# Gathered rows in one ring of 42, freed row by row, in place of seven buffers of six; the column products inside the next tile's sum

## The chip, the cores and the metric

The kernel runs on one core of a Trainium2 chip. The metric is the device time of one execution in microseconds (us); less is better. Engines are called by the profile's names: PE is TensorE (matmul; PEld is its weight load), DVE is VectorE, ACT is ScalarE, POOL is GpSimd, SP is SyncE.

## The reference

Two graph layers on 3327 nodes with 512 features; the adjacency matrix is random, symmetric, with some nine ones in a row. Cut to what matters:

```python
# layer 0: graph attention with 4 heads of 128 features
feats = einsum('nf,hfo->hno', x, W)
logits = lrelu(e_s[:, :, None] + e_n[:, None, :], 0.2) - 1e10 * (1 - adj)
out = relu(softmax(logits) @ feats + b)          # heads side by side
x1 = layernorm(x + out)
# layer 1: an attention sum and a plain sum over the same neighbours
gate_a = sigmoid([adj @ x1, x1] @ Wa.T + ba);  gate_b = sigmoid([adj @ x1, x1] @ Wb.T + bb)
e = where(adj != 0, exp(-leaky_relu(s_left[:, None] + s_right[None, :], 0.01)), 0)
x_a = (e / (sum(e) + 1e-5)) @ (x1 @ W_sa);  x_b = adj @ (x1 @ W_g) + b_g
out = layernorm(x1 + sigmoid(gate_a * x_a + gate_b * x_b))
```

## The kernel before

As few entries of the adjacency matrix are set, the kernel doesn't multiply by it. It has three stages.

**Lists (up to about 213 us).** It reads the matrix once, makes for each node a list of its neighbours' numbers, computes the features of all nodes into a table in HBM (`table0`, rows of 520 floats: 512 features and 8 more), and sorts the nodes by their number of neighbours, in two groups of 12 and 14 tiles of 128 nodes. So each tile `j` has a cap `CAPS[j]` on the neighbours of its nodes, from 14 down to 4. The first tile of a group (`T0`: tiles 0 and 12) has one row more, the "stair", for the few nodes with longer lists.

**Layer 0 (213 to 547 us).** For each tile, a gather is one indirect DMA on POOL's queue that brings one neighbour's row for each of the 128 nodes: 128 rows of 2080 bytes, 266 KB. `gather(table, j)` issues those of a whole tile. The rows go to buffers of `U` = 6 rows each, of which there are `GB` = 7 under one tag; a tile takes one to three of them, filled evenly, so that many are not full. In the second group a tile's first place is the node's own input row, fetched as a pair with its own table row from `own1` by one DMA. A buffer is given to a new tile once all reads of all its rows are done.

The tiles run in the order `order0`: 11, 10, 0 to 9, 23, 12, 24, 13, 22, 14, 21, 15, 20, 16, 19, 17, 18, 25. Step `i` of the loop at line 884 issues, in this order (each engine runs its own part in order, and the waits between engines and DMAs follow from the data):

- the gathers of the tile three steps ahead (`AHEAD`, line 887)
- `publish` of finished tiles, in groups of up to four: they are scaled by ACT and, with DVE's columns, written to `table1`, in the second group by a scatter on POOL's queue
- `columns2` of the tile two steps back: ACT copies its transposed row (`xt1`, line 842), and PE makes eight columns of products from it (`pcol`, line 845)
- `attend` of this tile: each gathered row is multiplied by its weights in place, two rows of three on DVE (line 815), every third (`s % 3 == 2`) on ACT (line 813), and PE adds it up in PSUM with an identity matrix (line 821)
- for the tile one step back: the sum plus input (line 899), transposes on PE (`columns1`, line 838), statistics for the layer norm; then `columns3`, the copy of the columns on DVE (line 849)
- `weigh_a` and `weigh_b` of the next tile: logits, softmax. Line 770 adds the logits' two parts and line 787 copies the neighbours' new numbers, each once for every part (buffer) of the tile, `got[j]`.

**Layer 1 (from 550 us).** The same with `table1`, in another order of tiles (short ones first, then long and short in turn, the two shortest last). Here DVE makes the weighted sum (line 1026) and adds some rows in pairs (line 1028, `paired`, counted within a part); PE adds rows and pairs (line 1047), turns the sums (line 1057) and multiplies them by the two weight matrices (line 1066). `weights_a` has one line 961, one line 970 and, after the first, one line 981 for each part of the tile. Finished rows are scattered to the output on POOL's queue (line 145) in groups.

Of the kernel before, what the change touches and what calls it, by code (L numbers as in the profile page):

```python
# [8 lines left out]
F32 = mybir.dt.float32  # L9
# [5 lines left out]
P = 128  # L15
# [9 lines left out]
S = 24  # L25
# [4 lines left out]
LW = 32  # L30
ND = 25
LEVELS = 4
U = 6
GB = 7
AT = 12
NCOL = 8
GRP = 4
# [42 lines left out]
def sparse_pass(  # L80
# [39 lines left out]
    nc = tc.nc  # L120
# [521 lines left out]
    m0 = tc.alloc_tile_pool(name="m0", bufs=2, side="left")  # L642
    ps = ctx.enter_context(tc.tile_pool(name="ps", bufs=1, space=PSUM))

    def gather(table, j):


        g, i = place(j)
        ahead = 0 if table is table1 else 1 + g
        c = CAPS[j] + ahead  # L650
        more = j in T0
        n = (c + more + U - 1) // U
        w = (c + more + n - 1) // n
        got = []
        for q0 in range(0, c + more, w):
            m = min(w, c - q0)
            buf = gp.tile([P, U, ROW], F32, tag="g", name=f"g_{nc.next_id()}", bufs=GB)
            for q in range(q0, q0 + m):
                s = q - ahead + 1
                if ahead == 2 and q < 2:  # L660
                    if q == 0:
                        nc.gpsimd.indirect_dma_start(
                            out=buf[:, 0:2, :].rearrange("p t w -> p (t w)"), out_offset=None,
                            in_=own1.rearrange("n t w -> n (t w)"),
                            in_offset=bass.IndirectOffsetOnAxis(ap=srt[g][:, i, S + 1 : S + 2], axis=0),
                        )
                    continue
                nc.gpsimd.indirect_dma_start(  # L668
                    out=buf[:, q - q0, :], out_offset=None, in_=table[:, :],
                    in_offset=bass.IndirectOffsetOnAxis(ap=srt[g][:, i, s : s + 1], axis=0),  # L670
                )
            o = 1 if ahead == 2 and q0 == 0 else 0
            if m > o:
                got.append((q0 + o - ahead + 1, m - o, buf, o))
        if more:
            stair[j] = buf[:, m, :]
            nc.gpsimd.indirect_dma_start(
                out=stair[j], out_offset=None, in_=table[:, :],
                in_offset=bass.IndirectOffsetOnAxis(ap=ids2[g][:, 0:1], axis=0),
            )  # L680
        return got

    stair = {}

    def to_nodes(pool, psum, name, cols):

# [72 lines left out]
        few, many = few[1:], many[1:]  # L759
    order0 += second[-1:]  # L760
    assert sorted(order0) == list(range(NT))
    got, ws, accs, ws2 = {}, {}, {}, {}

    def weigh_a(j):
        c = slots(j)
        g, i = place(j)
        w = ws[j] = m0.tile([P, S + 1, H], F32, tag="w", name=f"w{j}", bufs=3)
        es = srt[g][:, i : i + 1, S + 2 : S + 2 + H].bitcast(F32)
        for s0, n, buf, o in got[j]:
            nc.vector.tensor_add(w[:, s0 : s0 + n, :], buf[:, o : o + n, F : F + H], es.to_broadcast([P, n, H]))  # L770
        if j in T0:
            logit = m0.tile([P, H], F32, tag="logit", name=f"logit{j}")
            nc.vector.tensor_add(logit, stair[j][:, F : F + H], es2[g])
            small = psx.tile([P, B * H], F32, tag="pcol", name=f"to_nodes{j}", bufs=2)
            nc.vector.tensor_tensor(
                w[:, C0 + 1 :, :], to_nodes(m0, small, f"n{j}", logit),
                no_step.rearrange("p (b o) -> p b o", o=1).to_broadcast([P, B, H]), ALU.add,
            )
        nc.vector.scalar_tensor_tensor(w[:, :c], w[:, :c], 0.2, w[:, :c], ALU.mult, ALU.max)
        mx = m0.tile([P, 1, H], F32, tag="mx", name=f"mx{j}")  # L780
        nc.vector.tensor_reduce(mx[:, 0, :], w[:, :c].rearrange("p s h -> p h s"), AX.X, ALU.max)
        nc.vector.tensor_sub(w[:, :c], w[:, :c], mx.to_broadcast([P, c, H]))  # L782
        nc.scalar.activation(w[:, :c], w[:, :c], AF.Exp)  # L783

        for s0, n, buf, o in got[j]:
            a = max(s0, 1)
            nc.scalar.copy(srt[g][:, i, a : s0 + n], buf[:, o + a - s0 : o + n, F + H])
        if j in T0:
            nc.scalar.copy(ids2[g], stair[j][:, F + H : F + H + 1])
# [8 lines left out]
            small = psx.tile([P, B * H], F32, tag="pcol", name=f"to_rows{j}", bufs=2)  # L798
            ws2[j] = to_rows(m0, small, f"n{j}", w[:, C0 + 1 :, :])

    def attend(j, lean):


        w = ws[j]
        acc = accs[j] = ps.tile([P, F], F32, tag="acc", name=f"acc{j}", bufs=2)
        if not lean:
            nc.tensor.matmul(acc, ident, bias0, start=True, stop=False)
        for s0, n, buf, o in got[j]:
            for s in range(s0, s0 + n):
                gv = buf[:, o + s - s0, 0:F].rearrange("p (h o) -> p h o", h=H)  # L810
                if s % 3 == 2:
                    for h in range(H):
                        nc.scalar.activation(gv[:, h, :], gv[:, h, :], AF.Copy, scale=w[:, s, h : h + 1])  # L813
                else:
                    nc.vector.tensor_tensor(  # L815
                        gv, gv, w[:, s, :].rearrange("p (h o) -> p h o", o=1).to_broadcast([P, H, FO]), ALU.mult
                    )
                row = buf[:, o + s - s0, 0:F]
                if lean and s == 0:
                    nc.vector.tensor_add(row, row, bias0)  # L820
                nc.tensor.matmul(  # L821
                    acc, ident, row, start=(lean and s == 0), stop=(s == CAPS[j] and j not in T0)
                )
        if j in T0:
            gv = stair[j][:, 0:F].rearrange("p (h o) -> p h o", h=H)
            nc.vector.tensor_tensor(
                gv, gv, ws2[j].rearrange("p (h o) -> p h o", o=1).to_broadcast([P, H, FO]), ALU.mult
            )
            nc.tensor.matmul(acc, to_node, stair[j][:, 0:F], start=False, stop=True)
# [5 lines left out]
    def columns1(j):  # L835
        pt = turned[j] = psx.tile([P, KT, P], F32, tag="pt", name=f"x1t{j}", bufs=2)
        for k in range(KT):
            nc.tensor.transpose(pt[:, k, :], row1(j)[:, k * P : (k + 1) * P], ident)

    def columns2(j):  # L840
        xt1 = m0.tile([P, KT, P], F32, tag="xt1", name=f"xt1_{j}")
        nc.scalar.copy(xt1, turned[j])  # L842
        pcol = psx.tile([P, B * H], F32, tag="pcol", name=f"pcol{j}", bufs=2)[:, :NCOL]
        for k in range(KT):
            nc.tensor.matmul(pcol, xt1[:, k, :], v1[:, k, :], start=(k == 0), stop=(k == KT - 1))  # L845
        turned[j] = pcol
# [14 lines left out]
        else:  # L861
            scatter("table1", table1[:, :], own(j), row1(j), N - 1)

    AHEAD = 3
    for i in range(AHEAD):
        got[order0[i]] = gather(table0, order0[i])
    nc.sync.dma_start(own1[:, 0, :], xo)
    nc.sync.dma_start(own1[:, 1, :], table0[NG[0] * P : NP, :])
    psl.release()
# [12 lines left out]
    weigh_b(order0[0])  # L882
    ready = [[], []]
    for i in range(NT + 3):
        if i + AHEAD < NT:
            j = order0[i + AHEAD]
            got[j] = gather(table0, j)
        for args in ready[0]:
            publish(*args)
        ready = [ready[1], []]  # L890
        if 2 <= i < NT + 2:
            columns2(order0[i - 2])
        if i < NT:
            attend(order0[i], i >= 3)
        if 0 < i <= NT:
            j = order0[i - 1]
            y = row1(j)[:, 0:F]
            xj = y if j < NG[0] else got[j][0][2][:, 0, 0:F]
            nc.vector.scalar_tensor_tensor(y, accs[j], 0.0, xj, ALU.max, ALU.add)
            columns1(j)  # L900
            done = norm.add(i - 1, y)
            if done:
                k0, scale, shift = done
                ready[1] = [
                    (order0[k], scale[:, k - k0 : k - k0 + 1], shift[:, k - k0 : k - k0 + 1]) for k in range(k0, i)
                ]
        if 2 <= i < NT + 2:
            columns3(order0[i - 2])
        if 0 < i <= 7:
            sort1(rankis[1], 2 * i - 2, 2 * i)  # L910
        if i == 8:
# [156 lines left out]
    ends = {3, 7, 11, 15, 19, 22, 24, 25}  # L1068
    norm = Norm(m1, "n1", ends)
    at_ = lambda i: order[i] if 0 <= i < NT else None  # L1070
    for i in range(3):
        got[at_(i)] = gather(table1, at_(i))
    own_score(at_(0))
    weights_a(at_(0))
    weights_b(at_(0))
# [1 line left out]
    ready = None  # L1077
    for i in range(NT + 3):
        j, j1, jp, jpp = at_(i), at_(i + 1), at_(i - 1), at_(i - 2)
        if at_(i + 3) is not None:  # L1080
            got[at_(i + 3)] = gather(table1, at_(i + 3))
        if j1 is not None:
            own_score(j1)
        if jp is not None:
# [491 lines left out]
```

## Time and profile before

| | |
|---|---|
| median of 3 runs | 951.75 us (950.07 to 954.26) |
| the profiled execution | 953.83 us, its span 951.8 us |
| PE | 793.3 us busy, 83% of the span |
| DVE | 742.8 us, 78% |
| ACT | 279.0 us, 29% |
| POOL | 612.6 us, 64% |
| gathers of one row (line 668) | 464, 1035 ns each, 3.8 us from issue to landing |
| gathers of a pair (line 662), of a stair (line 677) | 14, 4 |
| granted PE clock, mean | 0.908 of full speed |

Shares of busy time are means over stages with different limits, so each stage has to be read by itself: the busy times in a stretch of time, the waits of one engine in it, and the timeline of that engine. In a row of groups the columns are: line, engine, operation, output and inputs, how often; then busy time in us and the mean of one in ns; then the idle time of the engine ahead of them, with what ended it ("issue" is idle time that no recorded event explains). In a timeline the columns are start in us, length in us, engine, line, operation, how often, and in brackets the idle time before it and what ended it. In a list of waits they are: who waited for whom, us in total, times, longest.

### The profile page before, as it was taken

What the parts mean: (1) busy time and instruction counts of PE and PEld (TensorE: products, weight loads), DVE (VectorE), ACT (ScalarE), POOL (GpSimd) and SP (SyncE); (2) the same over time, 40 slices, a digit from 0 to 9 for tenths busy, and PEclk for the clock granted to TensorE, in tenths of its full rate; (3) what the DMA queues carried; (4) which work ended last, traced back from release to release, by engine and by line L of the source; (5) the groups of instructions that cost most, each with busy time, mean ns of one, the idle gap of its engine ahead of it and who ended that gap; (6) DMA issues with size and microseconds to landing.
All of it is one profiled execution on the core that took longest, in us unless ns stands there. A gap on an engine that the chain in (4) does not pass through costs nothing.

```text
span 951.8 us, 10098 instructions
## 1 busy us (share of the span) xinstructions
PE 793.3 (83%) x2516; PEld 418.3 (44%) x2516; DVE 742.8 (78%) x2175; ACT 279.0 (29%) x820; POOL 612.6 (64%) x654
## 2 busy tenths in 40 slices
PE   4698987338999797799959749999989989899893
PEld 3476764114455444344434414444444434344341
DVE  4386888886987597487757839799999989999873
ACT  1121221004253254235343412213231222222241
POOL 6710154776677767767777477777777777777511
PEclk9798997558999898989989959999999999999997
DMA  8999899998678777877777266777676676667401
GB/s 334 374 366 396 336 328 391 383 384 282 180 201 256 211 237 225 299 240 226 225 223 232 106 179 190 200 188 190 190 197 190 189 192 192 190 188 188 138 23 47
DMA packets 71986, 221.41 MB, mean 233 GB/s; under 512 B 12912, under 2 KB 16960, under 8 KB 71024
## 3 DMA queue, kind: packets, MB, share of 16 engines
q0 software_dynamic: 46560, 153.64, 54.5%
q1 hardware_dynamic: 22704, 64.94, 18.0%
q10 hardware_dynamic: 2656, 2.10, 0.7%
q8 instruction: 23, 0.38, 0.2%
q14 instruction: 43, 0.35, 0.1%
HBM read 199.78 MB, written 28.32 MB: 240 GB/s over the span
## 4 chain that ended last, share of the span: by engine, by line
PE 44%; DVE 15%; DMA 15%; POOL 11%; issue 10%; ACT 3%; DVEq 0%; SPq 0%; POOLq 0%; ACTq 0%
PE acc L821 19%; PE pf L369 9%; POOL g L668 9%; DMA g<-table,srt 8%; DVE sw L1026 6%; PE po L1066 5%; DMA at<-in_adjB 5%; PE acc L1047 4%; PE pcol L845 2%; DVE g L1028 2%; DMA at<-in_adjL 1%; POOL out L145 1%; DMA a_row<-in_a_self 1%; PE sorted L548 1%; ACT za L1111 1%
## 5 line engine op out<-in xcount | busy, mean ns | idle before, releaser
L668 POOL DMA_INDIRECT g<-table,srt x464 | 480.2, 1035 | 159.0 <-issue 122.8
L821 PE MATMUL acc<-g,ident 128*128 128x512 f32 x504 | 239.1, 632 | 2.7 <-DVE g L815 1.6
L1026 DVE SCALAR_TENSOR_TENSOR sw<-g,e,sw 128x512 f32<-128x512 f32 x226 | 169.4, 750 | 12.4 <-ACT sw L1010 8.2
L821 PEld LDWEIGHTS acc<-g,ident 128*128 128x128 f32 x504 | 100.4, 203 | 123.8 <-issue 89.2
L1047 PE MATMUL acc<-g,ident 128*128 128x512 f32 x262 | 128.0, 617 | 23.0 <-DVE g L1028 13.3
L369 PE MATMUL pf<-w,xc 128*128 128x260 f32 x416 | 103.5, 412 | 13.6 <-DVE w L309 13.6
L815 DVE TENSOR_TENSOR g<-g,w 128x512 f32<-128x512 f32 x176 | 112.0, 694 | 0.6
L369 PEld LDWEIGHTS pf<-w,xc 128*128 128x128 f32 x416 | 84.7, 206 | 29.9 <-DVE w L309 14.1
L1066 PE MATMUL po<-wg,sT 128*128 128x512 f32 x208 | 96.6, 608 | 0.0
L1066 PE MATMUL po<-wsa,sT 128*128 128x512 f32 x208 | 94.7, 598 | 0.3 <-ACT sT L1059 0.3
L813 ACT ACTIVATE g<-g,w 128x128 f32<-128x128 f32 x304 | 91.6, 389 | 0.7 <-DVE w L796 0.7
L1047 PEld LDWEIGHTS acc<-g,ident 128*128 128x128 f32 x262 | 49.7, 195 | 93.6 <-issue 44.4
L1028 DVE TENSOR_TENSOR g<-g 128x512 f32<-128x512 f32 x95 | 65.7, 692 | 3.3
L379 POOL DMA_DIRECT2D table<-row x26 | 14.4, 553 | 80.1 <-ACT st L378 80.1
L1096 ACT ACTIVATE za<-za 128x512 f32<-128x512 f32 x26 | 16.4, 631 | 161.0 <-DVE za L1094 161.0
L1066 PEld LDWEIGHTS po<-wg,sT 128*128 128x128 f32 x208 | 40.7, 197 | 51.8 <-issue 50.8
L1066 PEld LDWEIGHTS po<-wsa,sT 128*128 128x128 f32 x208 | 40.0, 193 | 51.0 <-issue 48.5
L145 POOL DMA_INDIRECT out<-za,srt x26 | 29.1, 1121 | 49.3 <-ACT za L1111 43.3
L397 PE MATMUL pc<-at,pow 128*32 128x512 bf16 (+1 forms) x182 | 24.8, 412 | 40.8 <-DMA at<-in_adjB 24.6
L845 PE MATMUL pcol<-v,xt 128*128 128x8 f32 x208 | 29.8, 270 | 31.2 <-ACT xt L842 31.2
L783 ACT ACTIVATE w<-w 128x40 f32<-128x40 f32 (+10 forms) x26 | 6.2, 237 | 149.5 <-DVE w L782 149.5
L845 PEld LDWEIGHTS pcol<-v,xt 128*128 128x128 f32 x208 | 28.4, 209 | 37.8 <-ACT xt L842 36.6
(252 smaller groups left out, 931.6 us busy)
## 6 DMA issues: line engine op xcount, KB each, us to landing
at<-in_adjB SPq DMA_DIRECT2D x78, 512.0 KB, 11.7
g<-table,srt POOLq DMA_INDIRECT x464, 3.8
table<-row POOLq DMA_DIRECT2D x26, 260.0 KB, 6.3
xc<-in_xB SPq DMA_DIRECT2D x6, 1024.0 KB, 8.4
own<-in_xo SPq DMA_DIRECT2D x1, 3640.0 KB, 32.2
own<-table SPq DMA_DIRECT2D x1, 3640.0 KB, 48.7
at<-in_adjL SPq DMA_DIRECT2D x13, 256.0 KB, 13.3
table<-x1a SPq DMA_DIRECT2D x12, 260.0 KB, 4.2
```

Source lines behind the costliest of these rows:

```text
L145: put = nc.gpsimd.indirect_dma_start(out=dst, out_offset=bass.IndirectOffsetOnAxis(ap=rows, axis=0), in_=src, in_offset=None, bounds_check ...
L369: nc.tensor.matmul(pf[:, hh, :HC], xc[:, k, o : o + P], w0[:, k, hh, :], start=(k == 0), stop=(k == KT - 1))
L397: nc.tensor.matmul(pc[32 * c : 32 * c + 32, : nt * P], pow2[:, s, :], loaded[i, m], start=(s == 0), stop=(m + 1 not in ms or s == 3),)
L668: nc.gpsimd.indirect_dma_start(out=buf[:, q - q0, :], out_offset=None, in_=table[:, :], in_offset=bass.IndirectOffsetOnAxis(ap=srt[g][:, i ...
L813: nc.scalar.activation(gv[:, h, :], gv[:, h, :], AF.Copy, scale=w[:, s, h : h + 1])
L815: nc.vector.tensor_tensor(gv, gv, w[:, s, :].rearrange("p (h o) -> p h o", o=1).to_broadcast([P, H, FO]), ALU.mult)
L821: nc.tensor.matmul(acc, ident, row, start=(lean and s == 0), stop=(s == CAPS[j] and j not in T0))
L845: nc.tensor.matmul(pcol, xt1[:, k, :], v1[:, k, :], start=(k == 0), stop=(k == KT - 1))
L1026: nc.vector.scalar_tensor_tensor(sw, g[:, i, 0:F], e[:, s : s + 1], sw, ALU.mult, ALU.add)
L1028: nc.vector.tensor_add(g[:, i, 0:F], g[:, i - 1, 0:F], g[:, i, 0:F])
L1047: nc.tensor.matmul(plain[j], to, row, start=(not sums_of_two and i == 0), stop=(sums_of_two and i == len(rows) - 1),)
L1066: nc.tensor.matmul(proj[j], sT[:, k, :], wt[:, k, :], start=(half + k == 0), stop=(half + k == KT))
```

## The change

The seven buffers become one tile of 42 rows, `ring`. `plan` is called ahead for all tiles of a layer: it gives each row the next place, so that a tile's rows lie in one stretch, in two where the ring's end cuts it, and a pair never wraps (a place is left out for that). It puts the row's gather on a list. `gather()` issues gathers from that list as long as the row's place belonged to a tile that was freed; `free(j)` marks all rows up to tile `j` as free. Both are called in a step after the sum of the tile one step back is taken (in layer 1 at the head of the step). On the chip a gather still waits for the reads of the row that its place held before.

`columns2` is cut in two: ACT's copy (`columns2a`) stays ahead of `attend`, PE's products go into `attend`, behind the matmul of row 2.

```diff
-U = 6
-GB = 7
+RING = 42
...
-    def gather(table, j):
...
+    got, stair = {}, {}
+    ring = gp.tile([P, RING, ROW], F32, name="ring")
+    planned, freed = [0], [0]
+    waiting, ends_at = [], {}
...
+    def plan(table, j):
         g, i = place(j)
...
+        own_x_too = table is table0 and g == 1
+        first = 1 if table is table1 else 0
+        got[j] = []
+        s = first
+        while s <= CAPS[j]:
+            n = 2 if own_x_too and s == 0 else 1
+            if planned[0] % RING + n > RING:
+                planned[0] += 1
+            p = planned[0] % RING
+            m = min(CAPS[j] + 1 - s + n - 1, RING - p)
+            buf = ring[:, p : p + m, :]
+            got[j].append((s, m - (n - 1), buf, n - 1))
...
+            for k in range(k, m):
+                planned[0] += 1
+                waiting.append((planned[0], buf[:, k, :], table[:, :], srt[g][:, i, s : s + 1]))
+                s += 1
...
+        ends_at[j] = planned[0]
+
+    def gather():
+
+        while waiting and waiting[0][0] - freed[0] <= RING:
+            indirect(*waiting.pop(0)[1:])
+
+    def free(j):
+
+        freed[0] = ends_at[j]
...
-    def attend(j, lean):
+    def attend(j, lean, between):
...
                 nc.tensor.matmul(
                     acc, ident, row, start=(lean and s == 0), stop=(s == CAPS[j] and j not in T0)
                 )
+                if s == 2:
+                    between()
...
+    def columns2a(j):
+        xt1s[j] = m0.tile([P, KT, P], F32, tag="xt1", name=f"xt1_{j}")
+        nc.scalar.copy(xt1s[j], turned[j])
+
     def columns2(j):
-        xt1 = m0.tile([P, KT, P], F32, tag="xt1", name=f"xt1_{j}")
-        nc.scalar.copy(xt1, turned[j])
+        xt1 = xt1s[j]
...
-    AHEAD = 3
-    for i in range(AHEAD):
-        got[order0[i]] = gather(table0, order0[i])
+    for j in order0:
+        plan(table0, j)
+    gather()
...
     for i in range(NT + 3):
-        if i + AHEAD < NT:
-            j = order0[i + AHEAD]
-            got[j] = gather(table0, j)
         for args in ready[0]:
             publish(*args)
         ready = [ready[1], []]
-        if 2 <= i < NT + 2:
-            columns2(order0[i - 2])
+        third = order0[i - 2] if 2 <= i < NT + 2 else None
+        if third is not None:
+            columns2a(third)
         if i < NT:
-            attend(order0[i], i >= 3)
+            attend(order0[i], i >= 3, lambda: third is None or columns2(third))
+        elif third is not None:
+            columns2(third)
         if 0 < i <= NT:
...
             nc.vector.scalar_tensor_tensor(y, accs[j], 0.0, xj, ALU.max, ALU.add)
+            free(j)
+            gather()
             columns1(j)
...
-    for i in range(3):
-        got[at_(i)] = gather(table1, at_(i))
+    for j in order:
+        plan(table1, j)
+    gather()
...
-        if at_(i + 3) is not None:
-            got[at_(i + 3)] = gather(table1, at_(i + 3))
+        if i > 0 and jp is not None:
+            free(jp)
+        gather()
```

More of the change, by code (lines that the diff above doesn't have):

```diff
@@ L643, in sparse_pass @@
     ps = ctx.enter_context(tc.tile_pool(name="ps", bufs=1, space=PSUM))
-    def gather(table, j):
-        g, i = place(j)
[L649 to L681, printed above, removed]
@@ L683, in sparse_pass, with indirect @@
-    stair = {}
+    got, stair = {}, {}
+    ring = gp.tile([P, RING, ROW], F32, name="ring")
+    planned, freed = [0], [0]
+    waiting, ends_at = [], {}
+    def indirect(out_, table, ap):
+        nc.gpsimd.indirect_dma_start(
+            out=out_, out_offset=None, in_=table, in_offset=bass.IndirectOffsetOnAxis(ap=ap, axis=0)
+        )
+    def plan(table, j):
+        g, i = place(j)
+        own_x_too = table is table0 and g == 1
[10 more added lines that the diff above has]
+            got[j].append((s, m - (n - 1), buf, n - 1))
+            k = 0
+            if n == 2:
+                both = buf[:, 0:2, :].rearrange("p t w -> p (t w)")
+                planned[0] += 2
+                waiting.append((
+                    planned[0], both, own1.rearrange("n t w -> n (t w)"), srt[g][:, i, S + 1 : S + 2]
+                ))
+                k, s = 2, 1
+            for k in range(k, m):
+                planned[0] += 1
+                waiting.append((planned[0], buf[:, k, :], table[:, :], srt[g][:, i, s : s + 1]))
+                s += 1
+        if j in T0:
+            stair[j] = ring[:, planned[0] % RING, :]
+            planned[0] += 1
+            waiting.append((planned[0], stair[j], table[:, :], ids2[g][:, 0:1]))
+        ends_at[j] = planned[0]
@@ L761, in sparse_pass @@
     assert sorted(order0) == list(range(NT))
-    got, ws, accs, ws2 = {}, {}, {}, {}
+    ws, accs, ws2 = {}, {}, {}
     def weigh_a(j):
@@ L786, in weigh_a @@
             a = max(s0, 1)
+            if a == s0 + n:
+                continue
             nc.scalar.copy(srt[g][:, i, a : s0 + n], buf[:, o + a - s0 : o + n, F + H])
@@ L838, in columns1 @@
             nc.tensor.transpose(pt[:, k, :], row1(j)[:, k * P : (k + 1) * P], ident)
+    xt1s = {}
+    def columns2a(j):
+        xt1s[j] = m0.tile([P, KT, P], F32, tag="xt1", name=f"xt1_{j}")
+        nc.scalar.copy(xt1s[j], turned[j])
     def columns2(j):
-        xt1 = m0.tile([P, KT, P], F32, tag="xt1", name=f"xt1_{j}")
-        nc.scalar.copy(xt1, turned[j])
+        xt1 = xt1s[j]
         pcol = psx.tile([P, B * H], F32, tag="pcol", name=f"pcol{j}", bufs=2)[:, :NCOL]
```

## The prediction

> **What bounds the kernel now.** I read the busy table by stretches first, then GpSimd's waits in layer 0, its timeline, and the chain of waits. Layer 0's sums run from 213 to 547 us, layer 1's from 550 to 940. The busy times of three stretches (length, then PE, PEld, DVE, ACT, POOL, clock, DMA share, GB/s):
>
> ```profile
> 213.00:340.00 127.00, 118.06 (x334) 59.01 (x335) 97.23 (x271) 50.99 (x174) 89.37 (x90) 0.93 0.76 224
> 460.00:547.00 87.00, 68.25 (x216) 35.30 (x214) 62.29 (x199) 33.34 (x99) 58.82 (x59) 0.93 0.63 194
> 680.00:800.00 120.00, 113.32 (x307) 52.45 (x306) 111.52 (x256) 32.11 (x75) 93.98 (x86) 0.99 0.69 191
> ```
>
> TensorE fills the first stretch (118 of 127), nothing fills the second, TensorE and VectorE both fill the third. POOL looks idle everywhere, but a gather costs more than its busy time: each starts 0.30 us after the last ended, even when it waits for nothing. The groups of costliest instructions:
>
> ```profile
> L668 POOL DMA_INDIRECT g<-table,srt x464 | 480.2, 1035 | 159.0 <-issue 122.8
> ```
>
> So a row of gather costs 1.035 + 0.30, about 1.3 us (1.25 undisturbed), while TensorE sums a row in 0.86 (28 products in 12.0 us). Over layer 0 POOL is the slower one, and what it loses is not won back. What it lost there, by its waits between 173 and 547 us (total, times, longest):
>
> ```profile
> POOL g L668 <- PE acc L821: 9.5, 10, 4.3
> POOL g L668 <- DVE x1b L899: 5.5, 2, 3.1
> POOL g L668 <- ACT x1a L853: 4.4, 1, 4.4
> ```
>
> Less 0.30 each these are 6.5 + 4.9 + 4.1, with one odd gap of 0.35 about **15.8 us**, all waits for a buffer of six rows, at 216, 238, 336, 380, 404 and 410 us; none comes after 413. The chain of waits from 459 us on shows who pays:
>
> ```profile
> 515.54 3.94 DMA g<-table,srt
> ...
> 522.54 0.70 DVE g L820
> 523.29 8.85 PE acc L821 x20
> ```
>
> The last gather of tile 18 lands, its weights follow, and the sum starts: from here to the end of layer 0 everything hangs on that landing. Two tiles earlier it is the same (landing at 494, sum at 500). In layer 1 POOL loses only 2.6 us at the start; its gathers run at the 0.30 spacing from 550 to 889 us.
>
> **What the Trainium skill says.** "Perfetto Trace Analysis", section Optimization Strategy: a gap that repeats can mean that there is no room for the next tile. Here the trace agrees: the gaps above end with a reader that frees a buffer. The same page, Identifying Dependency Chains: an instruction that waits on several engines may get extra EventSemaphore instructions ahead of it. The trace has 91 of them before the 464 gathers of L668, most of 17 or 43 ns when nothing is late. "DMA: Bandwidth & Descriptors", Anatomy of one DMA, gives 2.0 us + bytes/436e3, for a gather of 266 KB an estimate of 2.6 us; the trace has 3.8 from issue to landing, which I use.
>
> **The change, part by part.**
>
> *Ring.* A row's gather waits for the row 42 places earlier. Take POOL's times of before less its waits, and TensorE's times of before as the release: ring row 42 would be gathered near 226, its place is free at 215; row 71 near 265, free at 253; row 107 (tile 8) near 310, free at 292; row 174 (tile 14) near 392, free at about 376. POOL trails by 8 us or more each time, so it never waits: -15.8 us of POOL's path by 413 us. Nothing is added to the gathers but waits (below).
>
> *Order on POOL.* Gathers are now issued after the sum of the step, up to 42 rows past the tile just freed, and publish's scatters of that step stand before them. Steps 18 and 22 scatter four tiles each. Before, the second four stood behind the last gather (523 us). Now they stand ahead of the last two or three rows of tile 18 and those of tile 25: the rows past tile 20 are 12 (tile 16) + 10 (19) + 11 (17) = 33, so only 9 of the 11 of tile 18 are issued by then (with places lost at wraps, fewer). Four scatters take 5.2 us (473.74 to 478.96). Their data come from a publish that follows the weights of tile 19, whose gathers land 15.8 earlier too, at 479; POOL gets to them near 497: no wait. So tile 18's last gather lands 15.8 - 5.2 = **10.6 us earlier**. SP's queue only has the two copies into own1 behind 42 instead of 29 first gathers, which another queue issues: nothing.
>
> *Column products.* TensorE stood 31.2 us before pcol (L845). Typical pieces of its timeline:
>
> ```profile
> 421.57 0.60 PE L838 MATMUL x1t<-ident,x1b 128*128 128x128 f32 x4
> 422.90 1.06 PE L845 MATMUL pcol<-v,xt 128*128 128x8 f32 x8 [0.73 <-ACT xt L842]
> ```
>
> After the change rows 0 and 1 (1.71 us) fill the 0.73; but row 2 is scaled by ScalarE after the same copy: copy 0.58 + four of 0.31, ready 1.97 after the transposes. 0.26 remains, so 0.47 a tile is saved, on some 14 tiles (in the five with sort1's products there was no gap): 6 us of TensorE. In tiles that wait for weights, pcol used to run during that wait; its 0.9 us now lie inside the sum. VectorE gets its columns (L849) three rows later, about 2 us, and the next tile's weights are queued behind: tiles of 5 to 8 rows may give 1 us each back. As TensorE waits for gathers at the end, all this cancels to nothing, except in tile 18, where the 0.9 is on the path and 0.5 comes back at tile 25. Layer 0: -10.6 + 0.4 = **-10 us**; if the scatters land behind tile 18, -15; if TensorE's losses reach the end, -5.
>
> *One stretch.* A layer 1 tile came in up to three parts, each with its own L961, L970 and all but the first L981 (49, 49 and 25 less 2 for the stairs). Laid out in 42 places there are 31 parts: 18 fewer. The rows say 0.22 + 0.16 + 0.16 us of busy time; start to start it is about 0.45: 18 x 0.45 = 8 us of VectorE, which sets the pace (111.5 of 120). But gathers come just in time: in the twelfth tile (tile 0, 14 rows) the last one lands 1.3 us before its weights, so of the 4 us saved up to there only 1 is kept; after it 8 parts, 3.6 us, are kept (later leads are 3.5 to 10 us). Layer 1: **-4 us**, from 0 to -8. Layer 0 loses 26 of 55 L770 (0.18 us) and as many casts, hidden by the wait for TensorE. Pairs stay at 95.
>
> *Waits, not shown before.* Each gather now waits for its own row's readers, so two or three semaphore waits may precede every gather. At nothing: the first gather of a buffer starts 0.30 after the last with its wait as without, as does a scatter, whose EVENT_SEMAPHORE and MOVE precede it (the one at 475.07 starts 0.30 after the one before). They run while the last gather is generated, 0.95 us. The other bound is in line: 2 x 43 ns x 482 gathers = +41 us; below zero nothing, as no wait is removed that cost anything but the 15.8. I take 0.
>
> **Sum.** -10 - 4 = -14. The profiled execution took 953.83 (span 951.8), so 939.8; it lies 2.1 above the median 951.75, which gives **938**, with 929 to 946 for this case.
>
> **Rivals.**
> 1. *The gain is smaller or gone*: POOL waits elsewhere, for the scatters' data or because TensorE, with VectorE's later columns, becomes the pace: against it, TensorE at full pace from 400 us on has 204 products of 0.43 and ten tiles' 1.6 us of the rest up to the end of tile 18, near 505, or 510 with VectorE's delays, instead of 532. Two scatter waits of 5 us take 10 away: 948.
> 2. *Slower: semaphores in line on POOL.* Price above, +41 us of POOL, which sets layer 0 (254 gathers, 22 us) and has 1 to 10 us of lead in layer 1. Against the 14 it decides from 0.03 us a gather. For it: every gather gets them; against: the constant 0.30. +41 - 14 = 27: 979.
> 3. *The change doesn't do row by row*: waits are kept for the ring as a whole, and each tile's weights wait for gathers two tiles ahead. A tile then takes its gathers (12 us), landing and sum (14) in turn, 26 x 12 us or so more in one layer: over 1200. Against it: x1a is also one tile with many rows, and L899 on one row waits for TensorE alone.
> 4. *More*: scatters fall behind tile 18 and layer 1 keeps its 8 us: -23, 929.
>
> **Chances.** Forecast 0.64, rival 1 0.14, rival 2 0.14, rival 3 0.03, rival 4 0.05. Range 929 to 954: it leaves out rivals 2 and 3 and takes in rival 1 with the time of before. About 0.5% (4.8 us) can be told from no change. Faster by more: 0.71; within: 0.11; slower: 0.18.
>
> **What would show it.** POOL's waits on L821, L899 and L853 in layer 0 gone; four scatters near 498, ahead of the last gathers; the last gather ends near 512 instead of 522.7; layer 1's first gather near 540 instead of 550.4; the wait of L845 below 10 us; L961 31 times. Wrong: a gap over 0.35 between POOL's gathers, POOL waiting at the first scatter of a step, or TensorE waiting on VectorE's products in tiles of 5 to 8 rows.

## The result, and the profile after

The changed kernel takes **946.21 us** (median of 11 runs, 944.53 to 947.82) beside 951.75 of the kernel before on the same chip: a ratio of 0.9942, 95% interval 0.9918 to 0.9965. It is 5.5 us faster, where 14 were forecast. The profiled execution took 945.74 us, its span 943.7. The spans of the two traces differ by 8.1 us, more than the medians: 0.8 of that lies ahead of layer 0's first sum, and the trace of the kernel before is 2.1 slower than its median.

Two marks split the span: the last gather of layer 0 (the one of tile 25's last row, on POOL) and the first gather of layer 1. Absolute times of two traces can't be compared in layer 0, since TensorE's first sum there starts anywhere from 207.9 to 212.6 us in the traces of this study; so I count from that sum. In us:

| | first sum to last gather | last gather to layer 1's first | layer 0 together | layer 1 to the end |
|---|---|---|---|---|
| before | 311.8 | 28.6 | 340.4 | 401.4 |
| after | 308.6 | 31.6 | 340.2 | 394.4 |
| forecast, after less before | -10.6 | +0.4 | -10 | -4 |
| measured, after less before | -3.2 | +3.0 | -0.2 | -7.0 |

So **the whole gain is layer 1's, and layer 0 gives nothing** that can be told. Three kernels below share the changed kernel's layer 0, instruction for instruction; theirs lasted 339.3, 339.3 and 342.1 us, so one trace tells layer 0 to about 1.5 us. Five share its layer 1, which lasted 393.8 to 394.4 us in four of them and 397.2 in the fifth.

First GpSimd's waits of the changed kernel, from 173 to 547 us (who waited for whom, us in total, times, longest):

```profile
POOL ring L650 <- issue: 37.5, 123, 0.3
POOL ring L650 <- DMA ring<-table,srt: 16.8, 55, 0.3
POOL ring L650 <- PE acc L835: 14.0, 46, 0.3
POOL ring L650 <- DVE x1b L920: 11.4, 2, 9.5
POOL table L144 <- DVE x1b L878: 10.3, 1, 10.3
POOL table L144 <- DVE shifted L877: 10.1, 1, 10.1
```

The old waits are gone: what is left behind PE or ScalarE is the 0.30 us between any two gathers. But a new one is there, 11.4 us in two pieces, 10.8 without the two times 0.30 (6.7 to 10.2 in the three other traces of this layer 0): gathers that wait for line 920, the residual sum (line 899 before). The two waits of L144 at the end are scatters behind the last gather, which wait for their data; the kernel before has 11.1 us of those. POOL's timeline of the changed kernel at the new wait:

```profile
380.91 0.94 POOL L650 DMA_INDIRECT ring<-table,srt  x1 [9.49 <-DVE x1b L920]
382.16 0.95 POOL L650 DMA_INDIRECT ring<-table,srt  x1 [0.30 <-PE acc L835]
...
391.66 0.94 POOL L650 DMA_INDIRECT ring<-table,srt  x1 [1.89 <-DVE x1b L920]
```

VectorE's timeline says what it waited behind:

```profile
372.62 0.68 DVE L829 TENSOR_TENSOR ring<-ring,w 128x512 f32<-128x512 f32 x1
373.33 0.69 DVE L834 TENSOR_TENSOR ring<-ring,bias 128x512 f32<-128x512 f32 x1
373.94 5.50 DVE L829 TENSOR_TENSOR ring<-ring,w 128x512 f32<-128x512 f32 x9
379.36 0.68 DVE L842 TENSOR_TENSOR ring<-ring,w_n 128x512 f32<-128x512 f32 x1
379.96 0.68 DVE L920 SCALAR_TENSOR_TENSOR x1b<-acc,ring 128x512 f32<-128x512 f32 x1
```

Line 920 of tile 23 adds that tile's own input row, which lies in the ring as the first half of its pair. PE had finished the tile's sum by 366.8 (its transposes for the tile before start there), but the step's program has VectorE do all the products of tile 12, the longest one, ahead of line 920. So the place of that one row stays taken to 380.6, and every later gather is behind the one that wants it. The kernel before stands for the same sum at nearly the same time, 172.6 us after the first sum and 171.8 in the changed one:

```profile
382.56 0.94 POOL L668 DMA_INDIRECT g<-table,srt  x1 [3.06 <-DVE x1b L899]
```

At this gather, the 152nd, the changed kernel's GpSimd was 16.3 us ahead of the kernel before, counted from the first sum. Five gathers later, behind its own wait, it is 7.5 ahead.

POOL's timeline at the end of layer 0, the scatters first and then the last gather of all:

```profile
503.71 1.02 POOL L144 DMA_INDIRECT table<-x1b,srt  x1 [0.30 <-issue]
...
507.64 0.98 POOL L144 DMA_INDIRECT table<-x1b,srt  x1 [0.30 <-issue]
...
517.75 0.94 POOL L650 DMA_INDIRECT ring<-table,srt  x1 [0.30 <-issue]
```

The four scatters stand ahead of tile 18's last rows and wait for nothing, as forecast. At the last gather ahead of them GpSimd is 8.5 us ahead of the kernel before, at the first one behind them 3.3: they cost 5.2. TensorE there, in the kernel before (the transposes of tile 17) and then in the changed one:

```profile
520.78 0.60 PE L838 MATMUL x1t<-ident,x1b 128*128 128x128 f32 x4
```

```profile
510.52 0.60 PE L854 MATMUL x1t<-ident,x1b 128*128 128x128 f32 x4
519.64 5.13 PE L835 MATMUL acc<-ring,ident 128*128 128x512 f32 x6 [8.52 <-DMA ring<-table,srt]
```

TensorE now reaches tile 18 early (tile 17's transposes at 510.52, before at 520.78) and waits 8.5 us for rows. Its first six products then take 5.13 us, at a mean granted clock of 0.53; six of the kernel called both below, after a wait of 3.01, take 2.84 at a clock of 1.00. That is 2.3 us on the path, and with the column products' 0.8, now inside this sum, it is about the 3.0 us by which the tail grew. The slow start is the larger part of it: in the kernel called columns_whole below, which has the column products ahead of the sum, the tail is 32.0 us as well, and the sum's 20 products take 11.40 us in place of 8.85.

Of the gathers' semaphores, the trace of after has (duration in ns: least, median, most):

```profile
L650 POOL DMA_INDIRECT ring<-table,srt x464: 940/947/1508, 170.6 to 885.2; - x155
L650 POOLq EVENT_SEMAPHORE  x445: 17/17/4009, 166.7 to 877.7; - x149
```

445 where there were 91, and the spacing of the gathers is still 0.30.

Layer 1 has two parts. Up to tile 13's scores (the sixth tile) VectorE waits for gathers, and that start is as long as before: 62.3 us from layer 1's first gather, 61.4 after. From there on the length follows VectorE's work. Its timelines of before and of after at that point, the last score of tile 13:

```profile
612.63 0.23 DVE L961 TENSOR_SCALAR e<-g,x1b 128x3 f32<-128x3 f32 x1 [4.79 <-DMA g<-table,srt]
```

```profile
610.68 0.23 DVE L984 TENSOR_SCALAR e<-ring,x1b 128x13 f32<-128x13 f32 x1 [3.94 <-DMA ring<-table,srt]
```

From these to the ends of the spans it is 339.2 us before and 333.0 after. The busy times of these two stretches (length; PE, PEld, DVE, ACT, POOL), before and then after:

```profile
613.00:952.00 339.00, 307.98 (x830) 143.28 (x828) 298.09 (x722) 96.26 (x221) 227.53 (x208) 0.96 0.59 165
```

```profile
611.00:944.00 333.00, 305.01 (x833) 141.34 (x831) 291.74 (x670) 94.81 (x221) 225.53 (x208) 0.98 0.60 168
```

VectorE has 52 instructions and 6.4 us of work less, and the stretch is 6.2 us shorter; its idle time is 41 us in both. So nearly all of the work counts. TensorE is busy for longer still (308 and 305 us), so these rows alone don't say which engine decides; the experiment on the parts does.

### The profile page after: what moved, and what is told of

Same layout as the page of the kernel before. It is cut to its first block, busy times and chain, and to the rows that moved or that the text cites. A ratio compares the mean times of both kernels' runs of the same rounds, so it can differ in the third digit from the quotient of the medians.

```text
span 943.7 us, 10295 instructions
## 1 busy us (share of the span) xinstructions
PE 783.3 (83%) x2516; PEld 409.0 (43%) x2516; DVE 733.8 (78%) x2095; ACT 275.7 (29%) x793; POOL 607.1 (64%) x654
## 5 line engine op out<-in xcount | busy, mean ns | idle before, releaser
L650 POOL DMA_INDIRECT ring<-table,srt x464 | 476.6, 1027 | 154.4 <-issue 62.2
L835 PE MATMUL acc<-ring,ident 128*128 128x512 f32 x504 | 246.7, 636 | 34.5 <-DVE ring L834 22.5
L1049 DVE SCALAR_TENSOR_TENSOR sw<-ring,e,sw 128x512 f32<-128x512 f32 x226 | 169.5, 750 | 11.7 <-ACT sw L1033 5.6
L835 PEld LDWEIGHTS acc<-ring,ident 128*128 128x128 f32 x504 | 97.0, 201 | 150.2 <-issue 77.9
L1070 PE MATMUL acc<-ring,ident 128*128 128x512 f32 x262 | 126.7, 613 | 20.2 <-DVE ring L1051 10.4
L829 DVE TENSOR_TENSOR ring<-ring,w 128x512 f32<-128x512 f32 x176 | 112.1, 694 | 0.6
L368 PE MATMUL pf<-w,xc 128*128 128x260 f32 x416 | 98.0, 396 | 13.8 <-DVE w L308 13.8
L368 PEld LDWEIGHTS pf<-w,xc 128*128 128x128 f32 x416 | 81.0, 197 | 28.3 <-DVE w L308 14.2
L827 ACT ACTIVATE ring<-ring,w 128x128 f32<-128x128 f32 x304 | 91.6, 390 | 1.0 <-DVE w L810 0.9
L1070 PEld LDWEIGHTS acc<-ring,ident 128*128 128x128 f32 x262 | 49.2, 193 | 90.2 <-issue 45.9
L1051 DVE TENSOR_TENSOR ring<-ring 128x512 f32<-128x512 f32 x95 | 65.7, 692 | 3.3
L144 POOL DMA_INDIRECT out<-za,srt x26 | 28.0, 1078 | 45.2 <-ACT za L1136 38.5
L372 ACT COPY row<-pf 128x512 f32<-128x512 f32 x26 | 15.2, 586 | 91.2 <-issue 45.6
L1082 ACT COPY sT<-pt 128x512 f32<-128x512 f32 x52 | 28.5, 587 | 34.7 <-PE pt L1080 34.3
```

The lines of the kernel that those rows point to most:

```text
L144: put = nc.gpsimd.indirect_dma_start(out=dst, out_offset=bass.IndirectOffsetOnAxis(ap=rows, axis=0), in_=src, in_offset=None, bounds_check ...
L368: nc.tensor.matmul(pf[:, hh, :HC], xc[:, k, o : o + P], w0[:, k, hh, :], start=(k == 0), stop=(k == KT - 1))
L650: nc.gpsimd.indirect_dma_start(out=out_, out_offset=None, in_=table, in_offset=bass.IndirectOffsetOnAxis(ap=ap, axis=0))
L829: nc.vector.tensor_tensor(gv, gv, w[:, s, :].rearrange("p (h o) -> p h o", o=1).to_broadcast([P, H, FO]), ALU.mult)
L835: nc.tensor.matmul(acc, ident, row, start=(lean and s == 0), stop=(s == CAPS[j] and j not in T0))
L1049: nc.vector.scalar_tensor_tensor(sw, g[:, i, 0:F], e[:, s : s + 1], sw, ALU.mult, ALU.add)
```

## The experiments

All are timed in five rounds beside the kernel before, which took 952.0 to 953.0 us, but for two batches that are told last.

**Theory A**: GpSimd's stream of gathers sets the end of layer 0, as forecast, and the 15.8 us that it no longer loses to buffers are lost to two other things: 10.8 us to own rows that line 920 holds, and 5.2 to the four scatters that moved ahead of the last gathers. This sum, -0.2, is the balance of the stream and not of layer 0. The last gather still came 3.2 us earlier, because the stream began 38.6 us ahead of the first sum in place of 36.6 and its gathers took 2.0 less in all; the tail's 3.0 then took that away. **Theory B**: TensorE with its columns inside the sums has become the bound, and GpSimd's waits only reflect it.

### The own row copied

ScalarE copies a second-group tile's own row to its place in `x1b` together with its weights, a tile ahead; line 920 reads it there, and the pair is free once TensorE and the weights are done with it.

```diff
+        if g == 1:
+            nc.scalar.copy(row1(j)[:, 0:F], got[j][0][2][:, 0, 0:F])
...
-            nc.vector.scalar_tensor_tensor(y, accs[j], 0.0, xj, ALU.max, ALU.add)
+            nc.vector.scalar_tensor_tensor(y, accs[j], 0.0, y, ALU.max, ALU.add)
```

> The changed kernel, and ScalarE copies a second-group tile's own row out of the ring with its weights (14 copies of 0.6 us), so that the late sum (L920) no longer holds a place of the ring. Theory A (GpSimd sets the end of layer 0: two waits for the row that L920 still reads cost it 10.8 us, and the four scatters ahead of tile 18's last gathers 5.2): both waits vanish, GpSimd gets to tile 18 up to 9 us earlier, TensorE's 8.5 us wait before tile 18's sum shrinks to 0-2, layer 1 starts 6 to 9 us earlier: 938 us. Theory B (TensorE with the column products inside the sum sets layer 0's end): 945 to 948.

Measured: 941.0 us, ratio 0.9879 (0.9851 to 0.9907). The profiled execution took 935.48, 5.5 less than the median, so the times of its trace make the edit look larger than the median does. In it no gather waits for the residual sum any more, the last gather starts 300.0 us after the first sum (308.6 in the changed kernel), and layer 0 takes 331.2. TensorE's timeline at tile 18:

```profile
509.50 5.00 PE L837 MATMUL acc<-ring,ident 128*128 128x512 f32 x6 [8.38 <-DVE ring L836]
```

Everything is 9 to 10 us earlier, TensorE's wait included: it comes early to tile 18 and waits as long as before. The product that it waits for is VectorE's, and VectorE had stood 7.19 us for a gather of this tile. So rows are late, and TensorE is not the bound. But theory A had expected this wait to shrink to 0 to 2 us, and it did not; the four scatters still stand ahead of these rows.

### The scatters behind the gathers

`publish` issues its scatters only after the step's `gather()`.

```diff
-            scatter("table1", table1[:, :], own(j), row1(j), N - 1)
+            put_later.append(j)
...
             free(j)
             gather()
+            put_now()
```

> The changed kernel with each step's scatters into table1 issued behind that step's gathers instead of ahead of them. Theory A: tile 18's last gather lands 5.2 us earlier, TensorE's wait before its sum falls from 8.5 to about 3.5 us, and layer 1 starts about 5 us earlier: 941 us. Theory B: no change (945 to 948), TensorE waits elsewhere instead.

Measured: 941.93 us, ratio 0.9888 (0.9857 to 0.9918). The last gather comes 305.4 us after the first sum, 3.2 earlier, and layer 0 takes 335.7. In POOL's waits those behind the residual sum (line 929 here) are still there, 10.8 us where the changed kernel has 11.4, and TensorE waits 2.8 us ahead of tile 18, where theory A had 3.5:

```profile
POOL ring L650 <- DVE x1b L929: 10.8, 2, 8.8
```

```profile
516.58 4.54 PE L835 MATMUL acc<-ring,ident 128*128 128x512 f32 x6 [2.79 <-DVE ring L834]
```

### Both

> The changed kernel with both edits: the tile's own row is copied to its node's row by ScalarE, so that the ring's pair is not held by the residual sum, and publish's scatters are issued behind the step's gathers. Theory A (GpSimd's stream sets the end of layer 0, and the two causes are separate pieces of that stream): the single edits moved layer 1's first gather by -10.2 and -3.65 us, so together it comes near 549.3 - 13.9 = 535.5, and the time is some 3.6 below that of the copied row alone: 941.0 - 3.6 = 937. Theory B (with GpSimd freed of one cause TensorE's own stream is what is left): no earlier than 539, and 941.

Measured: **932.03 us**, ratio 0.9776 (0.9752 to 0.9800). POOL's waits from 173 to 547 us, and TensorE at tile 18:

```profile
POOL ring L650 <- PE acc L837: 14.3, 45, 0.9
POOL table L144 <- DVE x1b L880: 9.2, 1, 9.2
```

```profile
509.05 2.84 PE L837 MATMUL acc<-ring,ident 128*128 128x512 f32 x6 [3.01 <-DVE ring L836]
```

The last gather comes 294.9 us after the first sum, **16.9 earlier than in the kernel before**, and the tail is 29.0: layer 0 takes 324.0. The 15.8 us of buffer waits are now really gone; one gather still waits 0.9 for TensorE. Ahead of tile 18's weights VectorE still stands 1.76 us for a gather, so the rows come last here too. Theory A stands, theory B does not.

The gain is larger than theory A's 937 and than the two edits' own sum: in the medians 5.2 and 4.3 us, 14.2 together; in layer 0 of the traces 9.0 and 4.5, 16.2 together. The surplus, 3 to 5 us, is no larger than the uncertainty of the four times that it is worked out from. One thing fits it: each edit alone leaves TensorE waiting over 8 us at some tile (8.38 above; 8.61 at 479 us with the scatters moved) and restarting slowly, while both together leave one wait of 5.2 at 472 us, with six products in 5.40, and at tile 18 a wait of 3.0 with six products in 2.84. That this makes the surplus was not tested.

### The column products

Two kernels have the products as a block ahead of the sum again: the changed kernel (columns_whole) and the one called both (both_whole). A third is the kernel before with the products moved alone (columns_alone).

```diff
             columns2a(third)
+            columns2(third)
         if i < NT:
-            attend(order0[i], i >= 3, lambda: third is None or columns2(third))
-        elif third is not None:
-            columns2(third)
+            attend(order0[i], i >= 3, lambda: None)
```

> The changed kernel with the column products as a block ahead of the next tile's sum, as before: the ring alone. Theory A: the products' place costs or brings nothing that reaches the end, since TensorE waits for tile 18's gathers anyway: 946, layer 1's first gather at 549.3 within 0.5. Theory B (TensorE's stream sets the end of layer 0): the bubbles of 26 steps come back, 31 us of waits of which those in the steps that TensorE bounds count, and the time goes up by 5 or more, to 951.

> The kernel called both (own row copied, scatters behind the gathers), with the column products as a block ahead of the next tile's sum. If GpSimd's stream still sets layer 0 there, the products' place is worth nothing: 932 within 2. If TensorE's stream has become the bound once GpSimd no longer stops, the bubbles of 26 steps come back in part: 936 or more. If the place inside the sum costs by itself, as the kernel before with the products moved alone (956.14 against 953.0) suggests: 928 to 929.

> The kernel before, with its seven buffers, but with the column products inside the next tile's sum. Theory A: TensorE runs up to a microsecond a step earlier, and so do the frees of the buffers that GpSimd waits for 15.8 us, four of them behind TensorE; a part of that comes off, 0 to 4 us: 948 to 952. Theory B (the column products made what layer 0 gained): 951.75 less the whole of layer 0's share, -1 to -5. Layer 1 is untouched and stays at 401.4 within 0.5 under both; if it does not, layer 1's length depends on how it is entered and not on its parts.

Measured: columns_whole 947.5 us (0.9931, 0.9908 to 0.9953), both_whole 931.87 (0.9777, 0.9751 to 0.9804): no difference from 946.21 and 932.03. columns_whole's trace has 338.1 us of layer 0 and 397.2 of layer 1, where the changed kernel's has 340.2 and 394.4; its layer 1 is the same program, so one trace can differ from the next by that much there too. What the move did to TensorE's waits in layer 0, in the changed kernel:

```profile
PE acc L835 <- DVE ring L834: 22.5, 7, 4.2
PE acc L835 <- DMA ring<-table,srt: 8.5, 1, 8.5
PE pcol L866 <- ACT xt L860: 1.5, 2, 0.7
```

Ahead of the column products 31.2 us of waits became 1.5, but 31.0 now stand ahead of the sums, which waited 2.6 before. TensorE's idle time was moved and not saved.

columns_alone takes 956.14, ratio 1.0047 (1.0028 to 1.0066): slower than the kernel before, a miss for both theories. Its last gather is 0.9 earlier (310.9), but its tail is 31.4 in place of 28.6; layer 0 is 1.9 longer, less than the 3 to 5 us that the times show. TensorE at its tile 18:

```profile
522.46 4.28 PE L821 MATMUL acc<-g,ident 128*128 128x512 f32 x6 [2.68 <-DVE g L820]
```

TensorE has closed its small gaps, comes early, waits, and takes 4.28 us for six products, at a granted clock of 0.66; then 1.1 us of column products are inside that sum. So the products' place brought nothing in any of the three, and in a layer that waits for gathers it can cost.

### Layer 1: the parts and the pairs

The weights of layer 1 are worked out over the old parts, 49 in place of 31 (old_parts), over the new parts with the rows paired and the sum cut by the old ones (old_pairs), and both (parts_and_pairs). Gathers and rows stay as they are.

```diff
+    def split_parts(j):
+        parts = [(s0, n, g, o) for s0, n, g, o in got[j]]
+        if len(parts) > 1:
+            return parts
+        s1, n1, g1, o1 = parts[0]
+        return [(s0, n, g1[:, s0 - s1 : s0 - s1 + n, :], 0) for s0, n in old_parts(j)]
...
-        for s0, n, g, _ in got[j]:
+        for s0, n, g, _ in split_parts(j):
```

> The changed kernel, but layer 1's weights (scores and gate sums) are worked out over the part sizes of the kernel before: 49 parts in place of 31, with rows, pairs and gathers as they are. If the 18 parts that went are what made layer 1 7.0 us shorter (18 x 0.45 = 8 on VectorE): layer 1, from its first gather to the end of the span, goes from 394.4 back to about 401.5, and the time to 953. If the gathers' new places or the pairs did it: layer 1 stays at 394.4 within 1, and the time at 946.

> The changed kernel, but layer 1 pairs its rows, and so cuts its sums in two, by the parts of the kernel before (in 11 of 26 tiles the pairs and the cut are others, the cut one to three rows later in eight or more of them), with 31 parts for the weights. The part sizes gave back 5.8 of the 7.0 us of layer 1. If the rest lies in the pairs: layer 1 at about 395.6, the time at 947 to 948. If the cut matters more than the parts: above 950. If neither: 946.2 within 1.5.

> The changed kernel with both the parts and the pairs of the kernel before in layer 1: but for the five tiles that the ring's end cuts, VectorE then has the same layer 1 as before, out of the ring. If parts and pairs each cost what they cost alone (5.8 and 3.4 us): 955, and layer 1's stretch from tile 13's scores to the end, 339.2 us before and 333.0 after, at 342. If they are two ways of making the same wait, or the pairs' 3.4 are a matter of their mixture with 31 parts: 952 to 953, and the stretch at 339.

| | time, us | ratio to before | layer 1 | tile 13's scores to the end |
|---|---|---|---|---|
| before | 951.75 | | 401.4 | 339.2 |
| after | 946.21 | 0.9942 (0.9918 to 0.9965) | 394.4 | 333.0 |
| old_parts | 952.01 | 0.9989 (0.9977 to 1.0001) | 400.6 | 337.8 |
| old_pairs | 949.63 | 0.9969 (0.9955 to 0.9983) | 398.4 | 336.8 |
| parts_and_pairs | 954.3 | 1.0016 (0.9998 to 1.0035) | 400.7 | 338.9 |

With both put back the gain is gone, and layer 1 is within 0.7 us of the kernel before. So the ring itself gives layer 1 nothing: the parts and the pairs are its gain. In the traces the parts give back 4.8 of the stretch's 6.2 us, the pairs alone 3.8, together 5.9, and these don't add up. But the same layer 1 gave 331.8 to 334.8 for this stretch in six traces, and the traces of old_parts and parts_and_pairs are of runs 4.1 us above and 2.5 below their medians. The ratios of the medians do add up: 0.47% or 4.5 us for the parts, 0.27% or 2.6 for the pairs, 0.74% or 7.0 for both, each to 2 or 3 us. So the parts' share is clear of this uncertainty, and the pairs' hardly.

What the pairs change is where a tile's sum is cut in two: the next tile's scores stand between the halves, and in the old parts a tile of nine rows was cut behind its ninth, with nothing left to lie beside ScalarE's exponentials. old_pairs has as much work on VectorE in the stretch as the changed kernel, and waits 2.8 us longer for ScalarE's first row (`sw`, 5.7 in place of 2.9). But the same line waits 2.1 for TensorE in the changed kernel and not here, and a wait in the tiles with a stair (line 715) is 2.0 longer, as it is in columns_whole, whose pairs are the new ones. So how the pairs cost what they cost stays open.

### Two batches that gave no reading

Five runs, four of them the first to be made, fell in two batches in which the kernel before itself took 1093 and 1108 us, with a mean PE clock of 0.85 to 0.86. There the own row copied, the scatters behind, both, and columns_whole took 1108.67, 1120.21, 1109.51 and 1101.92 us, and parts_and_pairs 1131.56. Four are 1.8 to 3.2% slower than the kernel before there; columns_whole's 1.1% is not clear (0.9981 to 1.0244). In their traces engines stand up to 33 us at a time with no recorded cause. The changed kernel itself was not run there, and there is no trace of the kernel before; no theory is judged by these runs, and all five kernels were run again as told above. Why everything is slower there, and whether the ring suffers more from it than the buffers, stays open. The chip's number settles nothing: the first four runs and the later parts_and_pairs have the same one, and beside the latter the kernel before took 952.58. What was expected of them:

> The changed kernel, and ScalarE copies a second-group tile's own row out of the ring with its weights (14 copies of 0.6 us), so that the late sum (L920) no longer holds a place of the ring. Theory A (in layer 0 GpSimd sets the end: it lost 10.8 us in two waits for the row that L920 still reads, and 5.2 us to the four scatters that now stand ahead of tile 18's last gathers): both waits on L920 vanish, GpSimd gets to tile 18 some 9 us earlier, TensorE's 8.5 us wait before tile 18's sum shrinks to 0-2, layer 1 starts 6 to 9 us earlier: 938 us. Theory B (TensorE with the column products inside the sum sets layer 0's end, the gathers follow it): under 2 us of change, 945 to 948.

> The changed kernel with each step's scatters into table1 issued behind that step's gathers instead of ahead of them. Theory A: tile 18's last gather lands 5.2 us earlier (511 instead of 516), TensorE's wait before its sum falls from 8.5 to about 3.5 us, and layer 1 starts about 5 us earlier: 941 us. Theory B: no change (945 to 948), TensorE waits elsewhere instead.

> Both edits of r1 and r2. Theory A: no wait of GpSimd in layer 0 but for scatters at its end, TensorE goes from tile 17 to tile 18 without a wait (8.5 us of wait and 2.4 us of slow products after it saved): layer 1 starts 10 to 11 us earlier, 935 us. If it is not better than r1, TensorE is the limit from there on. Theory B: 945 to 948.

> The changed kernel with the column products back in their old place, ahead of the tile's sum (the ring alone). Theory A: GpSimd sets the end of layer 0, so at most 1 us either way (0.9 us less of tile 18's sum, which then has its products in the wait): 945 to 947. Theory B: TensorE gets its gaps of 0.73 back and loses 0.47 on some 14 tiles, less the 0.9 in tiles that wait: 3 to 6 us slower or, if the later columns hold VectorE up, 2 to 4 us faster.

> The changed kernel with both the parts and the pairs of the kernel before in layer 1: but for the five tiles that the ring's end cuts, VectorE then has the same layer 1 as before, out of the ring. If parts and pairs each cost what they cost alone (5.8 and 3.4 us): 955, and layer 1's stretch from tile 13's scores to the end, 339.2 us before and 333.0 after, at 342. If they are two ways of making the same wait, or the pairs' 3.4 are a matter of their mixture with 31 parts: 952 to 953, and the stretch at 339.

## Why the prediction was wrong, by its own steps

- **"POOL trails by 8 us or more each time, so it never waits"** is the step that failed. The release of a place was taken from TensorE's sums at four sampled rows. The pair's first half is read once more, by line 899 (now 920), a step later on VectorE, behind the products of the next tile. The line stood in the waits of before, with 5.5 us; it was put down to the buffers of six and taken to go with them. In a ring one held row stops all that follow: 10.8 us. The forecast had named the sign of it, a gap over 0.35 between gathers; there are two, of 9.49 and 1.89.
- **The scatters** came where they were forecast, ahead of tile 18's last rows and without a wait for data, at 503.7 us in place of 498. Their price of 5.2 was right; moving them back brought 3.2 at the last gather and 4.5 in layer 0, and 5.1 at the last gather where the own row was copied as well (300.0 to 294.9).
- **"10.6 us earlier" for the last gather** became 3.2. With both holds taken away it is 16.9 earlier, so the 15.8 us were there to be had; the sum's first term was right, and a charge of 10.8 against it was missing.
- **The tail, +0.4,** was +3.0. The column products lie inside tile 18's sum as priced (0.8 of 0.9). But ahead of the sum they would not have run in that wait, as the forecast had it: in columns_whole they start behind it, at 517.15, after ScalarE's copy. What was left out is that an early TensorE waits, and starts again slowly: 5.13 us for six products in place of 2.84. The trace of before had such starts as well: behind a wait of 6.41 us, at 498 us, its column products took 1.88 us in place of 1.06. The Trainium skill has this on the page "TensorE: Matmul & The Clock Gate", section "HAM oscillation — how this bites in real kernels": after an idle gap of more than about 3.4 us TensorE starts over at a throttled clock. The traces agree at 8.52 and 8.38 us of wait (six products in 5.13 and 5.00, clock 0.53 and 0.55) and at 3.01 (2.84, clock 1.00). But waits of 2.79 and 2.68, shorter than that limit, were followed by 4.54 and 4.28 at a clock of 0.61 and 0.66, so the length of the last wait alone doesn't decide.
- **The column products: nothing in sum.** TensorE's wait ahead of them fell from 31.2 to 1.5 us, well below the 10 named, and stands ahead of the sums instead. That it is worth nothing was right for the ring, with or without the own row's edit; in the kernel before alone they cost 3 to 5 us.
- **Layer 1, -4,** was -7.0, inside its range of 0 to -8. The count of parts (31) and the work that goes were right: 18 parts at 0.45 are 8, and VectorE's work fell by 6.4 behind tile 13. Mis-sized was the share that counts. The forecast let gathers take back what is gained up to the twelfth tile; they set the pace only up to the sixth. The pairs' new places were not priced at all ("Pairs stay at 95" is true, and misses where they are).
- **Semaphores in line on POOL (rival 2)** are refuted: 354 more of them at an unchanged spacing of 0.30. Whole-tile waits (rival 3) are refuted by the time, as they meant over 1200. Rival 1, a smaller gain because POOL waits elsewhere, came closest: 948 against 946.21, for another wait than the scatters' data that it named.

## What to carry to other kernels

In a ring the last reader of each single row sets the pace of all that follow, so ask for every row who reads it last and what stands ahead of that reader on its own engine; a row that someone wants much later is copied out. Issue stores behind the gathers that the critical path waits for when both share a queue. Freeing one engine in a stage bound by another bought nothing here, and cost a slow restart; fewer, larger operations on the engine whose work sets the length counted nearly in full (6.2 of 6.4 us).

## What the runs showed of the hardware that was not expected

Extra semaphore instructions ahead of a gather cost GpSimd nothing that shows: with 445 in place of 91 the gathers still start 0.30 us after one another's end. TensorE's products ran at about half speed after waits of 8.4 to 8.5 us (six in 5.0 to 5.1 us, against 2.84, at a granted clock of 0.53 to 0.55), at a clock of 0.61 to 0.66 after waits of 2.7 to 2.8, and at 1.00 after one of 3.0.
